# Products of 64 by 64 in the statistics pass of a four-layer convolution kernel

## The chip, the cores and the metric

The kernel runs on one core of a Trainium2 chip. The metric is the device time of one execution in microseconds, as the median of several runs. Beside it there is one profiled execution, from which every duration below is taken; a profiled execution can take a little longer than the others.

## The reference

The input is 4 images of 16 channels, 512 by 512, float32. Four layers follow one another: a window attention block with a small MLP (layer 0), a quantised 3x3 convolution with batch normalisation (layer 1), two 3x3 convolutions with a residual (layer 2), and a 3x3 convolution with a 16-128-16 MLP and a residual (layer 3). The change concerns layer 1 alone:

```python
def _L1_conv_ref(x, weight, gamma, beta):
    xq = _fake_quant(x, 8, 1.0)            # round(x / step) * step, step = max|x| / 127
    wq = _fake_quant(weight, 8, 1.0)
    y = conv3x3(xq, wq)                    # 16 -> 16 channels, padding 1
    mean = jnp.mean(y, axis=(0, 2, 3))     # per channel, over all images and pixels
    var = jnp.var(y, axis=(0, 2, 3))
    inv = gamma * jax.lax.rsqrt(var + 1e-5)
    y = y * inv[None, :, None, None] + (beta - mean * inv)[None, :, None, None]
    return jnp.clip(y, 0.0, 6.0)
```

The mean and variance of y need the whole of y before any pixel can be normalised. So the kernel computes y twice: once for its statistics alone, and once more in the pass that goes on through layers 1 to 3.

## The kernel before

The kernel has three stages. `window_attention` computes layer 0 and writes its result x1 to device memory, with a running maximum of its magnitude in `peak`. The statistics pass, in the first half of `conv_layers`, reads x1 once, convolves it and keeps only sums. A long loop over t (the second half of `conv_layers`) reads x1 again and runs layers 1, 2 and 3 in a pipeline to the output. An `attention_block` for inputs that the first form can't take is in the program but is branched over here.

How rows are laid out: x1 is a tensor of M + 1 = 65 blocks, each of 128 partitions x 4 strips (S) x 512 columns. A quarter of the partitions, `_quad(b)` = partitions 32b to 32b + 31, belongs to image b; within it 2 neighbouring rows (a pair) x 16 channels. Block mm holds pair mm of each of the 4 strips of the image. A 3x3 convolution of a pair needs two neighbouring blocks, `side` 0 and 1, and three column shifts `dx`; the weights `cq[_quad(b), side, dx, :]` are a 32 x 32 matrix (2 rows x 16 channels in, 2 rows x 16 channels out), the same in each quarter, in bf16, made by `quant_weights`.

The statistics pass runs over mm = 0 to 63. For one step:

- `scaled(mm + 2)` (L996) multiplies a loaded block by 1/step and adds a rounding constant, in place, on GpSimd (POOL; the first two blocks on VectorE).
- `rounded(mm + 2)` (L999) subtracts the constant on ScalarE (ACT) and writes bf16 into one of the three buffers `qs`, each with a zero column at either end.
- `_conv_turn` (L909) issues the products. `_turns` lists 24 turns (2 sides x 3 shifts x 4 images i), and each turn has 4 products, one for each strip j: rows of image i in the partitions `_quad(i)`, the output in `p[i][_quad(j)]`. So a step has 96 products of a 32 x 32 weight with 32 x 512 data, six of them accumulated into each 32 partitions x 512 columns of PSUM. A product is two instructions on TensorE, a weight load (PEld in the profile) and a matmul (PE). p is one of two sets of four PSUM banks, in turn, so that bank p[i] holds image i, all four strips.
- four `bn_stats` on VectorE (DVE, L1024), one a bank, reduce 512 columns of each partition to statistics in `stats`.
- `load` (L892) fetches block mm + 8 on SP's DMA queue into one of eight flat tiles, which are the buffers y, xi and x of the later loop. It waits until `rounded` has read that tile.

After the last step `bn_aggr` combines the statistics of each partition, `over_strips` adds the partitions of one channel (partition number modulo 16) through a product with the matrix `same`, and scale and shift of the normalisation follow. Which image or strip a partition of `stats` came from doesn't matter, only its channel.

The order on TensorE, VectorE, ScalarE and SP is the order in which the program is written (`tc.manual_schedule`); semaphores between engines come from what each instruction reads and writes. The main loop uses `_conv_turn` and `cq` too, from `group` (conv `None`), for the second computation of y.

Of the kernel before, what the change touches and what calls it, by code (L numbers as in the profile page):

```python
# [1 line left out]

# [10 lines left out]
BF16 = mybir.dt.bfloat16  # L13
# [10 lines left out]
B, C, H, W = 4, 16, 512, 512  # L24
P = 128
# [88 lines left out]
def conv_chain(ctx: ExitStack, tc: tile.TileContext, x, xw, mats, vecs, cqs, cws, hots, out):  # L114
# [33 lines left out]
    with tc.If(safe == 0):  # L148
        attention_block(tc, x, x1, m, v, peak)
    conv_layers(tc, x1, out, cw, cq, sw, m, v, peak)  # L150


# [728 lines left out]
def _quad(i):  # L881
    return slice(32 * i, 32 * i + 32)
# [18 lines left out]
def _turns():  # L901

    return [(side, dx, i) for side in range(2) for dx in range(3) for i in range(4)]


def _conv_turn(nc, p, weights, src, side, dx, i):

    for j in range(4):
        nc.tensor.matmul(  # L909
            p[i][_quad(j)], weights[_quad(i), side, dx, :],  # L910
            src[side][_quad(i), j, dx : dx + W],
            start=side == 0 and dx == 0, stop=side == 1 and dx == 2,
        )
# [3 lines left out]
def conv_layers(ctx: ExitStack, tc, x1, out, cw, cq, sw, m, v, peak):  # L917
# [18 lines left out]
    nc = tc.nc  # L936
    ld = ctx.enter_context(tc.tile_pool(name="l3l", bufs=2))
    act = ctx.enter_context(tc.tile_pool(name="l3a", bufs=1))
# [7 lines left out]
    def ring(name, n, dt=F32):  # L946
        tiles = rings[name] = [
            act.tile([P, 4, WP], dt, name=f"{name}{i}") for i in range(n)
        ]
        return lambda mm: tiles[mm % n]  # L950
# [5 lines left out]
    qs = ring("q", 3, BF16)  # L956
# [31 lines left out]
    def load(mm, t=None):  # L988
        if t is None:
            t = ld.tile([P, S, W], F32, tag="x", name=f"tx{mm}")  # L990
        loaded[mm] = t
        _load_pairs(nc, loaded[mm], x1, mm)

    def scaled(mm, at=slice(0, S), engine=nc.vector):
        t = loaded[mm][:, at]
        engine.tensor_scalar(t, t, ix, ROUND, ALU.mult, ALU.add)  # L996

    def rounded(mm, at=slice(0, S)):
        nc.scalar.activation(  # L999
            inner(qs(mm))[:, at], loaded[mm][:, at], AF.Identity, bias=unround  # L1000
        )

    flat = [
        t.rearrange("p s x -> p (s x)")[:, 0 : S * W].rearrange("p (s x) -> p s x", x=W)
# [9 lines left out]
    for mm in range(M):  # L1016
        if mm + 2 <= M:
            scaled(mm + 2, engine=nc.gpsimd)
            rounded(mm + 2)
        p = banks[4 * (mm % 2) : 4 * (mm % 2) + 4]  # L1020
        for turn in _turns():
            _conv_turn(nc, p, cq, (qs(mm), qs(mm + 1)), *turn)
        for b in range(B):
            nc.vector.bn_stats(stats[:, mm * B + b, :], p[b])  # L1024
        if mm + AHEAD <= M:
            load(mm + AHEAD, flat[mm % AHEAD])
# [166 lines left out]
    for t in range(-2, M + 7):  # L1193
# [5 lines left out]
        mm = t - 4  # L1199
# [5 lines left out]
        mm = t - 3  # L1205
# [7 lines left out]
        mm = t - 1  # L1213
# [4 lines left out]
        mm = t  # L1218
# [135 lines left out]
```

## Time and profile before

| | |
|---|---|
| median of 3 runs | 6459.06 us (6456.72 to 6465.38) |
| the profiled execution | 6479.63 us, span 6477.8 us |
| mean granted TensorE clock, whole span | 0.979 |
| TensorE busy, whole span | 6215.1 us, 96% |
| VectorE, ScalarE, GpSimd busy | 3208.4, 4062.8, 130.9 us |
| pairs of weight load and matmul | 146,976, of these 6144 in the statistics pass |
| end of the last product of the attention stage, start of the first of the statistics pass | 3541.8 us, 3577.3 us |
| last matmul of the statistics pass | begins at 3829.9 us |
| mean granted TensorE clock, 3577.2 to 3830.5 us | 0.71 |
| bytes moved and DMA share, 3577.2 to 3830.5 us | 267 GB/s, 0.71 |

Times within the span are counted from its start. "PE busy" is the union of the time in which matmuls were in flight; many are in flight at once, so that it doesn't tell how full the array is. "clock" is the share of TensorE's full clock that was granted. In the groups of instructions the columns are: line, engine, operation, what is written and read, rows*columns of the weight, count, then busy us and mean ns of one, then idle us of the engine before them with what ended it. "issue" is time in which the engine waited for nothing that the profile shows. A line of the DMA view is a queue: packets, MB, share of the time of 16 DMA engines.

### The profile page before, as it was taken

What the parts mean: (1) busy time and instruction counts of PE and PEld (TensorE: products, weight loads), DVE (VectorE), ACT (ScalarE), POOL (GpSimd) and SP (SyncE); (2) the same over time, 40 slices, a digit from 0 to 9 for tenths busy, and PEclk for the clock granted to TensorE, in tenths of its full rate; (3) what the DMA queues carried; (4) which work ended last, traced back from release to release, by engine and by line L of the source; (5) the groups of instructions that cost most, each with busy time, mean ns of one, the idle gap of its engine ahead of it and who ended that gap; (6) DMA issues with size and microseconds to landing.
All of it is one profiled execution on the core that took longest, in us unless ns stands there. A gap on an engine that the chain in (4) does not pass through costs nothing. (4 is left out here: it accounts for less than half of the span.)

```text
span 6477.8 us, 317011 instructions
## 1 busy us (share of the span) xinstructions
PE 6215.1 (96%) x146976; PEld 3422.4 (53%) x146976; DVE 3208.4 (50%) x4713; ACT 4062.8 (63%) x5602; POOL 130.9 (2%) x89
## 2 busy tenths in 40 slices
PE   8999999999999999999998569999999999999999
PEld 4555555555555555555553335555555555555554
DVE  3444444444444444444443564555555555555555
ACT  4777777777777777777775443444444444444444
POOL 0000000000000000000000520000000000000000
PEclk9999999999999999999998679999999999999999
DMA  3333333333333333333232752222222222222221
GB/s 80 62 72 61 72 61 72 61 72 61 72 61 72 60 73 61 72 60 73 59 58 36 295 181 75 83 82 82 83 84 86 81 81 81 81 86 82 83 74 51
DMA packets 568966, 515.30 MB, mean 80 GB/s; under 512 B 349008, under 2 KB 480208, under 8 KB 547152
## 3 DMA queue, kind: packets, MB, share of 16 engines
q1 hardware_dynamic: 567344, 494.52, 29.4%
q8 instruction: 1154, 18.91, 1.2%
q14 instruction: 180, 1.47, 0.1%
q10 hardware_dynamic: 288, 0.39, 0.0%
HBM read 225.87 MB, written 134.48 MB: 56 GB/s over the span
## 5 line engine op out<-in xcount | busy, mean ns | idle before, releaser
L1139 PE MATMUL tb<-y,mat 32*32 32x512 f32 x16384 | 1494.9, 596 | 6.5 <-issue 6.0
L1145 ACT ACTIVATE hid<-tb,vec 128x512 f32<-128x512 f32 x1280 | 829.5, 688 | 1068.3 <-PE tb L1139 1066.1
L368 ACT ACTIVATE e<-pair 128x1024 f32<-128x1024 f32 x1024 | 992.3, 1021 | 225.7 <-PE pair L360 225.0
L296 PE MATMUL pair<-x,taps 32*32 32x512 f32 x18432 | 968.2, 606 | 1.8 <-ACT y L307 1.2
L1147 DVE TENSOR_SCALAR hid<-tb,vec 128x512 f32<-128x512 f32 x768 | 574.4, 748 | 745.1 <-PE tb L1139 737.3
L417 PE MATMUL bank<-y,fc_e 32*32 32x512 f32 x8192 | 878.5, 607 | 3.7 <-ACT hid L422 3.1
L422 ACT ACTIVATE hid<-bank,f1b 128x512 f32<-128x512 f32 x1024 | 679.4, 686 | 298.4 <-PE bank L417 284.7
L352 DVE COPY yt<-bank 128x512 f32<-128x512 f32 x512 | 353.7, 691 | 905.6 <-PE bank L347 905.6
L360 PE MATMUL pair<-g,y 32*128 32x128 f32 x16384 | 652.1, 285 | 39.7 <-ACT e L368 38.7
L909 PE MATMUL tb<-z,cw 32*32 32x512 f32 x12864 | 634.6, 599 | 5.3 <-issue 4.1
L360 PEld LDWEIGHTS pair<-g,y 32*128 32x128 f32 x16384 | 541.4, 186 | 186.0 <-ACT e L368 108.8
L296 PEld LDWEIGHTS pair<-x,taps 32*32 32x32 f32 x18432 | 459.2, 103 | 288.5 <-issue 183.6
L1139 PEld LDWEIGHTS tb<-y,mat 32*32 32x32 f32 x16384 | 464.1, 103 | 270.7 <-issue 152.5
L909 PE MATMUL tb<-h,cw 32*32 32x512 f32 x12672 | 571.1, 597 | 3.5 <-ACT z L1078 1.5
L909 PE MATMUL tb<-q,cq 32*32 32x512 bf16 x12672 | 424.2, 458 | 151.3 <-issue 98.9
L909 PE MATMUL tb<-x,cw 32*32 32x512 f32 x12480 | 562.5, 597 | 2.0 <-ACT z L1078 1.4
L379 PE MATMUL bank<-e,yt 128*32 128x128 f32 x16384 | 555.3, 276 | 0.9 <-ACT r L394 0.9
L384 PE MATMUL bank<-e,hot 128*32 128x512 f32 x4096 | 534.4, 592 | 0.0
L379 PEld LDWEIGHTS bank<-e,yt 128*32 128x32 f32 x16384 | 417.7, 109 | 108.1 <-DVE yt L352 52.8
L1155 PE MATMUL tb<-hid,mat 128*32 128x512 f32 x4096 | 452.7, 594 | 0.0
L430 DVE TENSOR_TENSOR xo<-bank,y 128x512 f32<-128x512 f32 x256 | 177.0, 691 | 546.6 <-PE bank L428 544.7
L347 PEld LDWEIGHTS bank<-mat,y 128*128 128x128 f32 x2048 | 215.1, 141 | 430.1 <-issue 376.5
(158 smaller groups left out, 6731.7 us busy)
## 6 DMA issues: line engine op xcount, KB each, us to landing
x<-in_xw_dram SPq DMA_DIRECT2D x32, 2600.0 KB, 10.2
y<-y SPq DMA_DIRECT2D x2048, 32.0 KB, 2.1
tx<-x SPq DMA_DIRECT2D x64, 1024.0 KB, 5.7
xi<-x SPq DMA_DIRECT2D x1024, 64.0 KB, 2.1
out_dram<-xi SPq DMA_DIRECT2D x64, 1024.0 KB, 5.9
x<-xo SPq DMA_DIRECT2D x2000, 32.0 KB, 1.7
y<-x SPq DMA_DIRECT2D x24, 1024.0 KB, 5.5
xi<-x SPq DMA_DIRECT2D x24, 1024.0 KB, 5.2
```

The lines of the kernel that those rows point to most:

```text
L296: nc.tensor.matmul(bank(u)[quad(vv)], taps[quad(u), tap, :], xts[n // 2][quad(u), vv, dy : dy + WS, at : at + BW], start=tap == 0, stop=ta ...
L360: nc.tensor.matmul(bank(u)[:, P * jj : P * jj + P], y2[quad(u), vv, jl + jj].rearrange("p w t -> p (w t)"), g[quad(u), vv, jl + jj].rearra ...
L368: nc.scalar.activation(e[:, 2 * i : 2 * i + 2].rearrange("p u j t -> p u (j t)"), pairs[i], AF.Exp,)
L379: nc.tensor.matmul(b[quad(u), P * jj : P * jj + P], yt[:, jj, quad(u)], e[:, u, jj, :], start=True, stop=True,)
L384: nc.tensor.matmul(d[quad(u)], own, e[:, u].rearrange("p j t -> p (j t)"), start=True, stop=True,)
L417: nc.tensor.matmul(b[quad(k)], fc1[quad(vv), quad(k)], y[quad(vv), u, :], start=True, stop=True,)
L422: nc.scalar.activation(hd, b, AF.Gelu, bias=f1b)
L909: nc.tensor.matmul(p[i][_quad(j)], weights[_quad(i), side, dx, :], src[side][_quad(i), j, dx : dx + W], start=side == 0 and dx == 0, stop= ...
L1139: nc.tensor.matmul(p[_quad(c)], w1[_quad(b), 1 - par, 32 * c : 32 * c + 32], inner(ys(mm + par))[_quad(b), s, :], start=True, stop=True,)
L1145: nc.scalar.activation(hd, p, AF.Relu, bias=v("l3_b1"))
L1147: nc.vector.tensor_scalar(hd, p, v("l3_b1"), 0.0, ALU.add, ALU.max)
L1155: nc.tensor.matmul(p[_quad(b), :], w2[:, par], hd, start=par == 0, stop=par == 1)
```

## The change

The products of the statistics pass are formed over 64 rows and 64 columns. A new tile `cqs` holds, for each side and dx, a 64 x 64 matrix in each half of the partitions: the weights of one image in rows and columns 0 to 31, the same weights for the next image in rows and columns 32 to 63, and zeros elsewhere. It is filled once, by a memset and four copies on VectorE, just before the first loads of the pass.

A product takes two images at once (h picks images 0, 1 or 2, 3), one strip (2i + c), and writes 64 partitions, c picking the lower or upper half, of bank p[2h + i]. A step has 2 x 3 x 2 x 2 x 2 = 48 products instead of 96. A bank then holds two images of two strips in place of one image of four strips; each partition still belongs to the same channel as before. The main loop, the loads, the scaling, the rounding and the bn_stats are as they were. All else in the kernel is unchanged.

```diff
+import itertools
...
+    cqs = act.tile([P, 2, 3, 64], BF16, name="cqs")
+    nc.vector.memset(cqs, 0.0)
+    for i in range(4):
+        at = 32 * (i % 2)
+        nc.vector.tensor_copy(cqs[_quad(i), :, :, at : at + 32], cq[_quad(i)])
...
         p = banks[4 * (mm % 2) : 4 * (mm % 2) + 4]
-        for turn in _turns():
-            _conv_turn(nc, p, cq, (qs(mm), qs(mm + 1)), *turn)
+
+
+        for side, dx, i, h, c in itertools.product(range(2), range(3), *[range(2)] * 3):
+            nc.tensor.matmul(
+                p[2 * h + i][64 * c : 64 * c + 64], cqs[64 * h : 64 * h + 64, side, dx, :],
+                (qs(mm), qs(mm + 1))[side][64 * h : 64 * h + 64, 2 * i + c, dx : dx + W],
+                start=side == 0 and dx == 0, stop=side == 1 and dx == 2,
+            )
         for b in range(B):
             nc.vector.bn_stats(stats[:, mm * B + b, :], p[b])
```

## The prediction

> **What bounds the kernel now.** I read the page's strip of 40 slices first. TensorE is at 9 or 8 tenths everywhere but in slices 22 and 23 (each 162 us), and there the clock drops and the DMA rises. That is the statistics pass, the only place that the change touches.
>
> ```profile
> PE   8999999999999999999998569999999999999999
> PEclk9999999999999999999998679999999999999999
> DMA  3333333333333333333232752222222222222221
> ```
>
> The view of the weight tile `cq` puts its first matmul at 3577.3 us and the last at 3829.9, so with that one's 0.6 the pass takes 253.2 us for 64 steps (`mm`): 3.96 us a step. Next, the busy time by stage (busy and count of each engine, clock, DMA share, GB/s), in the part with saturated loads and the steady part:
>
> ```profile
> 3600.00:3620.00 20.00, 12.07 (x464) 7.72 (x444) 10.21 (x17) 9.07 (x5) 15.90 (x9) 0.51 1.01 417
> ...
> 3620.00:3815.00 195.00, 112.95 (x4688) 74.07 (x4657) 120.50 (x196) 96.30 (x49) 92.90 (x51) 0.73 0.69 255
> ```
>
> No engine is full in the steady part: TensorE 113 of 195 us, VectorE 120, and the DMA at 0.69 moves 255 GB/s where it moved 417 just before. So something waits on a latency. The groups of this pass say for whom:
>
> ```profile
> L1024 DVE BATCH_NORM_STATS2 h<-tb 128x6 f32<-128x512 f32 x256 | 158.6, 684 | 96.5 <-PE tb L909 95.8
> L909 PE MATMUL tb<-q,cq 32*32 32x512 bf16 x6144 | 150.0, 534 | 138.5 <-issue 98.9 <-ACT q L999 38.9 <-DVE h L1024 0.4
> L999 ACT ACTIVATE q<-y,unround 128x2048 bf16<-128x2048 f32 x25 | 49.5, 2002 | 79.1 <-PE tb L909 37.8 <-DVE y L996 37.7 <-POOL y L996 3.3
> ```
>
> VectorE and ScalarE wait for TensorE, and TensorE for "issue", nothing that the profile shows (the 38.9 on ScalarE is the start, almost all before the pass's first matmul). TensorE's timeline shows the rhythm:
>
> ```profile
> 3605.19 3.65 PE L909 MATMUL tb<-q,cq 32*32 32x512 bf16 x128 [3.07 <-issue]
> 3611.40 3.64 PE L909 MATMUL tb<-q,cq 32*32 32x512 bf16 x128 [2.57 <-issue]
> 3617.34 3.60 PE L909 MATMUL tb<-q,cq 32*32 32x512 bf16 x128 [2.29 <-issue]
> 3622.46 2.06 PE L909 MATMUL tb<-q,cq 32*32 32x512 bf16 x128 [1.52 <-issue]
> ```
>
> It stops after exactly 128 matmuls, although a step has 96: the stops belong to the instruction stream, not to the data. The DMA view gives the reason. On the page the instruction queue moved 18.91 MB in 1154 packets, 16.4 KB each. A product is a weight load and a matmul; all 146,976 such pairs are 293,952 instructions, and 18.91 MB over the 317,011 of the program is some 60 bytes each, so 128 pairs fill one packet. Packet times put the stops to the wait for such a packet:
>
> ```profile
> q8 instruction: 1154, 18.91, 1.2%
> ...
> q8 instruction: 37, 0.61, 1.2%
> ```
>
> The second line is 3620 to 3815: 37 packets, and 4688 / 128 = 36.6 blocks of matmuls. So a block costs 195 / 36.6 = 5.3 us, however long its arithmetic takes. With no loads in flight (after 3815) blocks start 3.5 to 4.0 us apart, with saturated loads (3593 to 3617) 5.9 to 6.2, at most 7.3 (3800.11 to 3807.43): instruction packets queue behind 1 MB loads. This is a reading of timings, not a wait that the profile names.
>
> **The change part by part.** (1) *Removed: half the pairs.* 64 steps x 96 = 6144 become 64 x 48 = 3072, 48 blocks become 24. At 5.3 to 6.2 us a block, fetching needs 2.0 to 2.3 us a step instead of 4.0, and it goes on while a block runs: at light load the packet starts about 1.06 us after the first matmul of the block before. So it stops being the bound if a block's arithmetic lasts longer than its fetch.
>
> (2) *Added: array time.* Full and half clock show in two stretches of one block (of these products alone: TensorE, weight loads, VectorE, then clock, DMA share, GB/s):
>
> ```profile
> 3617.40:3620.40 3.00, 3.00 (x128) 2.23 (x128) 0.00 (x0) 0.50 0.96 399
> ...
> 3655.70:3657.30 1.60, 1.60 (x127) 1.47 (x128) 0.00 (x0) 1.00 0.74 302
> ```
>
> At clock 1.00 a whole block is 2.06 us, of which 0.37 is the last matmul's own length; seven intervals between eight waves of 16 plus the starts in the last wave make the other 1.68, some 0.216 us a wave. At 0.50 it is 3.64 with 0.63 for the last: 0.431 a wave. A 64x64 product fills four of the sixteen sub-blocks, so a step is 48 / 4 = 12 waves instead of 96 / 16 = 6: 2.59 us at full clock, 5.17 at half. The trace has no 64x64 product. Bounds: four abreast at the bf16 wave, 216 / 4 = 54 ns each, from below; from above the row of 128x32 products, which also run four abreast but in f32:
>
> ```profile
> L1155 PE MATMUL tb<-hid,mat 128*32 128x512 f32 x4096 | 452.7, 594 | 0.0
> ```
>
> 452.7 us / 4096 = 110 ns, hence 48 x 110 = 5.3 us. I take 54, the row of the same type and line; that L1155 overlaps four products of 594 ns at 110 each tells me that column tiles of one row group run side by side.
>
> (3) *The clock.* It is 0.71 over the pass, since TensorE idles two fifths of it. Stages where TensorE is 99% busy (1000 to 1100, 5000 to 5100) have 0.99 to 1.00. With 12 waves a step TensorE has no pause unless something else stops it, so I take 1.00 after the first steps. From 3577.3 the first two run cold in part: conv(0) 5.2 us, conv(1) about 3, so 8.2 together.
>
> (4) *What is late next.* VectorE's four bn_stats took 2.49 us in a row (3685.81), and a set of banks is needed again two steps later; a 1 MB load (1.049 MB at the 420 GB/s of 3577 to 3620) 2.50; ScalarE's rounding 2.00; GpSimd's scaling 1.97. All lie just under 2.59. Rounding of mm+2 can begin when conv(mm-1) has read its third buffer, and is needed in the second half of conv(mm+1): some two steps for 2.0 us. SP's loads go out after the rounding, eight steps ahead; nothing moves on SP or POOL. A block is 128 / 48 = 2.67 steps, 6.9 us at full clock, against 5.9 to 6.2 for a fetch under saturated loads: hidden by 0.7 to 1.0. If it were not, each further us costs 0.37 a step. With three servers within 4% of each other I add 0.11 for the times when one is late: 2.70 a step.
>
> (5) *Building cqs on VectorE:* a 128x384 memset and four 32x192 copies. The memset of 128x512 f32 took 485 ns, the 32x32 copies 172: about 1.4 us in all. They stand before the quantisation step; VectorE then sat idle for 3.74 us until 3573.85 for the first load, so they cost nothing; without that cover, 1.4 us.
>
> *Sum.* 8.2 + 62 x 2.70 = 175.6 us for the pass in place of 253.2: 77.6 off. The profiled execution took 6479.6 (span 6477.8), so 6402 by its own time. The median, 6459.1, is 20.5 below it. If the profiler's cost lies outside this pass the median falls to 6381.5; if all of it sits in this pass, which is bound by a DMA latency, only 57 are to be had, 6402. I take 74 off: 6385.
>
> [...]
>
> **The rivals.**
> (a) *The fetch stays the bound.* Loads would now run at 0.97 of the DMA instead of 0.69, and packets might wait as long as in the worst interval, 8.4 us (3584.95 to 3593.31). Then 8.4 / 2.67 = 3.15 a step, 8.2 + 62 x 3.15 = 203, 50 off: 6409. For it: the spread of 4.0 to 7.3. Against: the saturated stretch had 5.9 to 6.2.
> (b) *The clock stays mixed*, at 0.71: 2.59 / 0.71 = 3.65 a step, 234 us, 19 off: 6440. For it: any stop of 2 us brought 0.5 for some us. Against: the busy stages.
> (c) *Slower: the clock stays at half, or the tiles run two abreast.* One price: 5.17 us a step, 331 in place of 253, 78 on: 6537. It decides from 3.96 us a step, 330 ns for a wave of four. For it: the pass starts at 0.50, and kept it for 20 us (3600 to 3620); no 64x64 row. Against: there TensorE was idle 40% of the time, and at half clock it would be the only bound and never idle, the state in which every other stage shows 1.00.
> (d) *The change does not touch the bound:* if the stops were set by data loads, a step would stay near 3.96, and the time within a few us of 6459. Against: stops every 128, and a DMA at 0.69.
>
> **How the numbers follow.** Forecast 0.75, (a) 0.11, (b) 0.03, (c) 0.08, (d) 0.03. Below, the loads set the limit: 2.50 a step is 90 off, 6369; I begin at 6368. Above, (a) with a little of the profiler's share: 6413. Slower by over 0.2% (13 us; about what this kernel's runs can tell) is (c) and a part of (d): 0.09; within 0.2%: 0.03; faster 0.88.
>
> **What would show it.** Matmuls `q,cqs` x3072, 64x512, at a median near 375 to 400 ns; 12 waves near 216 ns; clock near 1.00 from about 3590; "issue" before them under 20 us instead of 98.9; the pass ending near 3753; loads at about 0.95 of the DMA; VectorE's bn_stats almost back to back; 24 instruction packets fewer. Wrong if the clock stays under 0.8, if waves of four take over 300 ns, or if stops after 128 pairs last 2 us and more.

## The result, and the profile after

The changed kernel takes 6390.38 us (median of 4 runs, 6387.1 to 6395.64) against 6462.22 for the one before (4 runs, 6456.72 to 6470.9): 71.8 us less, ratio 0.9888 with a 95% interval of 0.9871 to 0.9906. The forecast was 6385.

The page's strips of the changed kernel, 40 slices of 160 us, in tenths:

```profile
PE   8999999999999999999999789999999999999999
PEclk9999999999999999999999899999999999999999
DMA  3333333233323233333322752222222222222221
```

The dip in slices 22 and 23 is almost gone from TensorE and its clock; what is left is the time between the stages, before the first load has arrived and after the last statistics. Two stretches of the pass (busy and count of TensorE, weight loads, VectorE, ScalarE, GpSimd; clock, DMA share, GB/s):

```profile
3590.00:3620.00 30.00, 30.00 (x562) 21.26 (x558) 28.76 (x47) 23.27 (x12) 23.82 (x13) 1.00 1.01 419
...
3660.00:3700.00 40.00, 40.00 (x745) 30.47 (x741) 38.44 (x62) 30.82 (x16) 30.76 (x16) 1.00 1.01 419
```

TensorE is full at clock 1.00, VectorE at 96%, and the DMA moves 419 GB/s where it moved 255. TensorE's whole pass is now two lines of its timeline:

```profile
3570.23 6.25 PE L1030 MATMUL tb<-q,cqs 64*64 64x512 bf16 x72 [35.41 <-ACT q L1000]
3579.52 162.44 PE L1030 MATMUL tb<-q,cqs 64*64 64x512 bf16 x3000 [3.04 <-ACT q L1000]
```

After 1.5 steps it waits 3.04 us for a block that ScalarE is still rounding, and then 3000 products run without one gap: no stop after 128. The groups say the same (idle before, and what ended it), and so does the instruction queue on the page, with 24 packets fewer than 1154:

```profile
L1030 PE MATMUL tb<-q,cqs 64*64 64x512 bf16 x3072 | 168.7, 379 | 38.5 <-ACT q L1000 38.5
L1036 DVE BATCH_NORM_STATS2 h<-tb 128x6 f32<-128x512 f32 x256 | 159.5, 686 | 14.3 <-PE tb L1030 7.8
```

```profile
q8 instruction: 1130, 18.51, 1.3%
```

"issue" is no longer among what TensorE's matmuls wait for, and VectorE's wait for them fell from 95.8 to 7.8 us.

Where the time went, from the two traces: the pass from 253.0 to 171.7 us (81.3 less), what follows it from 2647.6 to 2647.1, and the pass began at 3570.2 instead of 3577.3. Those last 7.1 us lie in code that the change doesn't touch; in the executions below with full loads the pass began anywhere from 3573.9 to 3581.9. So the spans differ by 88.8, the medians by 71.8: the first profiled execution of the kernel before was a long one.

### The profile page after: what moved, and what is told of

The parts are those of the page before. It is cut to its first block, busy times and chain, and to the rows that moved or that the text cites. A ratio compares the mean times of both kernels' runs of the same rounds, so it can differ in the third digit from the quotient of the medians.

```text
span 6389.0 us, 310874 instructions
## 1 busy us (share of the span) xinstructions
PE 6228.6 (97%) x143904; PEld 3444.3 (54%) x143904; DVE 3210.5 (50%) x4718; ACT 4065.0 (64%) x5602; POOL 130.9 (2%) x89
## 5 line engine op out<-in xcount | busy, mean ns | idle before, releaser
L396 DVE TENSOR_TENSOR o<-bank,r 128x512 f32<-128x512 f32 x512 | 354.4, 692 | 141.5 <-ACT r L395 122.6
```

## The experiments

For each run, from its trace: pairs of weight load and matmul in a step, the pass from the first matmul's start to the last one's end, the mean step after the third, and the mean distance of the starts of blocks of 128 pairs where TensorE stops after them. Each experiment is one execution. The kernel before, executed beside them, took 6469.1 to 6475.3 us, and its two profiled passes below differ by 7.3 us, so a few us more or less in a pass mean nothing.

| run | pairs a step | pass, us | step, us | block, us |
|---|---|---|---|---|
| before | 96 | 253.0 | 3.96 | 5.29 |
| after | 48 | 171.7 | 2.60 | no stops |
| before_again | 96 | 245.7 | 3.86 | 5.19 |
| split256 | 96 | 245.4 | 3.76 | 5.41 |
| split128 | 192 | 428.9 | 6.61 | 4.57 |
| before_quarter | 96 | 196.2 | 3.05 | 4.18 |
| before_strips | 96 | 260.3 | 4.07 | 5.41 |
| half_products | 48 | 162.9 | 2.53 | two stops, 1.8 us in all |
| after_quarter | 48 | 169.4 | 2.60 | no stops |

**The kernel before, once more.** No edit.

> The kernel before, unchanged, profiled a second time. The first profiled execution took 6479.6 us where its other runs had a median of 6462. If the statistics pass is what varies (a latency that depends on what else the DMA does), this execution differs from the first by the length of its pass, which was 253.2 us; if the difference lay elsewhere, the pass is again 253 within 3 us and the attention stage, which ended 7 us later in the first than in the changed kernel, gives the rest.

It took 6464.8 us, 14.8 less than the first profiled execution. The pass was 7.3 us shorter and the loop after it 12.0 (2635.6), while the pass began 4.3 us later. So neither answer held alone: about half of the first execution's excess lay in the pass. Against this execution the changed pass saves 74 us rather than 81.

**The count put back, with the array time of the changed kernel.**

```diff
-        for side, dx, i, h, c in itertools.product(range(2), range(3), *[range(2)] * 3):
+        for n, side, dx, i, h, c in itertools.product(
+            range(2), range(2), range(3), *[range(2)] * 3
+        ):
+            at = 256 * n
             nc.tensor.matmul(
...
+                p[2 * h + i][64 * c : 64 * c + 64, at : at + 256],
+                cqs[64 * h : 64 * h + 64, side, dx, :],
+                (qs(mm), qs(mm + 1))[side][
+                    64 * h : 64 * h + 64, 2 * i + c, at + dx : at + dx + 256
+                ],
...
```

> The changed kernel with each 64x512 product cut into two of 256 columns: 96 pairs of weight load and matmul in a step again, the same array time (24 waves of half the length, about 2.6 us a step at full clock), the same tiles. Theory, the instruction packets set the pace: a block of 128 pairs is again 1.33 steps, its arithmetic some 3.5 us against 5.3 to 6.2 us for a packet, so TensorE stops after each 128 and a step takes about 4.0 us, the pass some 255 us. Rival, the wide tiles or the steady clock did it and the count doesn't matter: 2.6 to 2.7 us a step, pass 172 to 180 us, no stops.

The pass took 245.4 us, where the unchanged kernel's run above took 245.7: the whole gain is gone with the same wide tiles. TensorE's timeline and the busy time of a stretch (columns as above) of this run:

```profile
3702.06 3.70 PE L1033 MATMUL tb<-q,cqs 64*64 64x256 bf16 x128 [1.69 <-issue]
3707.45 3.70 PE L1033 MATMUL tb<-q,cqs 64*64 64x256 bf16 x128 [1.69 <-issue]
3711.74 10.92 PE L1033 MATMUL tb<-q,cqs 64*64 64x256 bf16 x384 [0.59 <-issue]
3724.90 5.36 PE L1033 MATMUL tb<-q,cqs 64*64 64x256 bf16 x128 [2.23 <-issue]
```

```profile
3620.00:3800.00 180.00, 137.87 (x4572) 127.56 (x4576) 119.00 (x192) 94.77 (x48) 94.38 (x48) 0.96 0.79 284
```

The groups hold 128 or a multiple of 128, and after each TensorE waits for "issue". Three blocks in a row without a stop (x384 in 10.9 us) show that a packet can be in time at 3.6 us a block; on the average it isn't. The clock is 0.96 here, against 0.71 in the kernel before, and the pass is no shorter: the low clock doesn't make the stops. That the stops make the low clock is likely, but no rule comes out of it: in the kernel before, each of the 26 stops of 2.07 us or more was followed by a mean clock of 0.67 or less in the next 4 us, in this run 5 of the 10 such stops. This fells the rival that wide tiles or a steady clock made the gain.

**192 pairs a step.** As above with `range(4)` and 128 columns.

> The changed kernel with each product cut into four of 128 columns: 192 pairs in a step, the array time in streaming unchanged. Theory, packets of 128 pairs set the pace: 1.5 blocks a step; the loads then need only half the DMA's time, so a block comes every 4.2 to 5.4 us, 6.3 to 8.1 us a step, twice that of 96 pairs. Rival, the loads or something else per step sets the pace: near 4 us as with 96 pairs.

6.61 us a step, inside the theory's range and far from the rival's 4. The stops of this run:

```profile
3706.67 2.00 PE L1033 MATMUL tb<-q,cqs 64*64 64x128 bf16 x128 [2.02 <-issue]
3711.51 3.05 PE L1033 MATMUL tb<-q,cqs 64*64 64x128 bf16 x128 [2.84 <-issue]
```

At full clock a block has 2.00 us of arithmetic here, like the 2.06 of 32x32 products, and as many instructions, and it starts 4.57 us after the one before. With the loads at 146 GB/s it is shorter than the 5.2 to 5.4 of 96 pairs.

**Fewer bytes to queue behind.** The loads of the pass cut to one strip of four; the other strips hold a constant that rounds to zero.

```diff
+        if quarter:
+            s = int(mm == M)
+            nc.sync.dma_start(t[:, 0:1], x1[mm - s * M, :, s : s + 1])
+            return
...
+        nc.vector.memset(flat[mm][:, 1:S], ROUND)
...
-            scaled(mm + 2, engine=nc.gpsimd)
+            scaled(mm + 2, slice(0, 1), engine=nc.gpsimd)
```

> The kernel before, with the loads of the statistics pass cut to one strip of four (256 KB in place of 1 MB; the other three strips are filled once with the rounding constant, so that they round to zero), the scaling cut to that strip, and all 96 products of a step kept. Theory, instruction packets queue behind the loads: blocks of 128 pairs come every 3.5 to 4.0 us as where no loads were in flight, 2.6 to 3.0 us a step, and TensorE still stops after 128. Rival, the instruction stream is slow by itself: 5.3 us a block and 4.0 us a step, unchanged.

```profile
3705.73 2.06 PE L909 MATMUL tb<-q,cq 32*32 32x512 bf16 x128 [2.51 <-issue]
3709.47 2.23 PE L909 MATMUL tb<-q,cq 32*32 32x512 bf16 x125 [1.69 <-issue]
...
3713.49 3.27 PE L909 MATMUL tb<-q,cq 32*32 32x512 bf16 x128 [1.19 <-issue]
```

The step fell from 3.86 to 3.05 with every product kept, and TensorE's timeline still stops after 128 (the second block's last three products waited 0.20 us for VectorE and stand in the line left out). So the loads lengthen the wait and don't make it: with a quarter of the bytes a block still costs 4.18 us, a little over the 4.0 that I took for the upper end (and 3.05 a step over 3.0).

**The same bytes in smaller rows.** Each load as four DMAs of a strip (`t[:, s]` from `x1[mm, :, s]`).

> The kernel before, with each load of the pass issued as four DMAs of one strip: rows of 2 KB in place of 8 KB, the same bytes. If an instruction packet waits behind a number of data packets, packets of a quarter of the size let it through sooner: blocks of 128 pairs near 4.2 us as with quarter loads, 3.1 us a step. If it waits behind bytes that are queued, whatever their pieces: 5.2 us a block, 3.9 us a step, unchanged.

The packets did become smaller, as the DMA view of 3620 to 3780 says (23439 in place of 5782 on the loads' queue for the same 42 MB):

```profile
DMA packets 23472, 43.18 MB, mean 270 GB/s; under 512 B 2603, under 2 KB 2603, under 8 KB 23439
...
q1 hardware_dynamic: 23439, 42.68, 83.2%
```

The block took 5.41 us and the step 4.07, no less than in the two runs of the kernel before (5.29 and 5.19, 3.96 and 3.86). So an instruction packet doesn't wait behind a fixed number of data packets; waiting by bytes fits. More than that these runs don't show of the queue.

**Half the products, 32x32 as before.** Only side 0; the products of side 1 are left out.

> The kernel before, with only the 48 products of side 0 in a step, 32x32 as before; the products of side 1 are left out. Theory: a block of 128 is 2.67 steps, a packet of 5.9 to 6.2 us under saturated loads gives 2.2 to 2.3 us a step, so the loads (2.50 us) and VectorE (2.49) set the pace: 2.5 to 2.6 us a step, with three waves of arithmetic only, and loads near 420 GB/s. Rival, a wait in each step (a semaphore, a buffer) rather than in each 128 instructions: stays between 3.5 and 4.0 us.

```profile
3600.00:3740.00 140.00, 85.80 (x2656) 37.73 (x2671) 136.50 (x223) 110.40 (x55) 109.03 (x58) 0.50 1.01 418
```

2.53 us a step, as the theory had it. This stretch ran at half clock throughout and with TensorE busy 61% of the time, and still a step took 2.5: the loads at 418 GB/s or VectorE at 97% set it, and the run doesn't part the two. What it leaves out halves the array time together with the count, so by itself it can't say which of the two matters; the two runs above that cut the products finer change the count and keep the array time nearly as it is. The step of 2.53 is the floor under the changed kernel, and 64 x (2.60 - 2.53) is under 5 us; I tried no version for it.

**What paces the changed kernel.** Its loads cut to a quarter, as above.

> The changed kernel with the loads of the pass cut to one strip of four (256 KB; the other strips hold the rounding constant and round to zero) and the scaling cut to that strip; all 48 products kept. Theory, TensorE's twelve waves now set the pace: 2.59 to 2.60 us a step, unchanged, at a quarter of the DMA's rate. Rival, the loads (2.50 us at 420 GB/s, the DMA busy throughout) set it: the step falls to VectorE's 2.4 to 2.5 us or lower.

```profile
3600.00:3730.00 130.00, 130.00 (x2410) 99.08 (x2406) 124.84 (x201) 101.68 (x51) 35.91 (x52) 1.00 0.40 106
```

2.60 us a step at 106 GB/s, as with full loads: TensorE's twelve waves set the step, and not the loads, though in the changed kernel they keep the DMA busy 1.01 of the time.

**The same products where packets are in time.** The main loop's second convolution with 64x64 products too.

```diff
...
+            elif wide:
+                side, dx, j, h = next(pairs)
+                for c in range(2):
+                    nc.tensor.matmul(
+                        conv_banks[2 * h + j][64 * c : 64 * c + 64], cqs[64 * h : 64 * h + 64, side, dx, :],
+                        conv[1][side][64 * h : 64 * h + 64, 2 * j + c, dx : dx + W],
...
-        weights = cq if layer is None else cw[:, layer]
+        weights = cqs if layer is None else cw[:, layer]
```

> The changed kernel with the 64x64 products also in the main loop's second computation of the quantised convolution (68 turns of it, 48 pairs in place of 96; a bank then holds other images and strips than the next layer takes it for). There blocks of 128 pairs already last 4.9 to 5.1 us at 83 GB/s of data, so packets are in time. Theory: array time counts, six more waves of 0.216 us a turn, and 68 x 1.3 = 88 us more than the changed kernel's main loop (2636 to 2647 us from the end of the pass), more still if TensorE loses time between products of 32 and of 64 rows, which alternate there. Rival, the main loop too is paced by its instruction stream, or half the count is worth having everywhere: 3264 fewer pairs at 5.0 us for 128 are 125 us less.

It took 6727.03 us, against 6472.0 for the kernel before beside it. The loop after the pass took 2978.9 us instead of 2639.9 (after_quarter, the same loop). The sign was the theory's, the size four times as large. Its timeline shows why:

```profile
5016.19 1.06 PE L1151 MATMUL tb<-y,mat 32*32 32x512 f32 x8
5017.18 0.41 PE L1192 MATMUL tb<-q,cqs 64*64 64x512 bf16 x4
5017.52 1.06 PE L1151 MATMUL tb<-y,mat 32*32 32x512 f32 x8
5018.51 0.41 PE L1192 MATMUL tb<-q,cqs 64*64 64x512 bf16 x4
```

The second column is how long a group was in flight: each begins when the one before is all but over (the second at 5017.18, the first ends at 5016.19 + 1.06 = 5017.25). With one size, in the changed kernel, products of the two lines share the array: four `q,cq` products begin at 5031.11 us while 18 of the hidden layer's last until 5031.69, and the next of those begin at 5031.31, before the four end at 5031.52. With two sizes they take turns, each group beginning some 0.07 us before the end of the one before. Two more runs tested that: the sets of hidden products first, and the wide ones after them, so that the size changes twice in a turn instead of ten times; and the narrow products in that order as a control.

```diff
             conv(None, qs, mm, done0, mm) if -2 <= mm <= M + 1 else None,
-            (t - 5, 1) if 0 <= t - 5 < M else None, [], EARLY,
+            (t - 5, 1) if 0 <= t - 5 < M else None, [], range(8),
```

> As the kernel with 64x64 products in the main loop too, but in that group the eight hidden sets (32x32 products in f32) are issued first and the 24 turns of 64x64 products after them, so that the two sizes change once in a group instead of ten times; the output is again that of other strips. That kernel's main loop took 2979 us, 340 more than the 2640 of the others, where array time gave 88. Theory, TensorE does not overlap products of one size with those of another, and each change of size costs: the loop comes back to the time of the narrow kernel in the same order plus 88 to 130 us. Rival, the 64x64 products are themselves dear beside f32 work: still 300 us and more above the narrow one.

> Control for the run above: the changed kernel with 32x32 products in the main loop, the group's hidden sets first and its conv turns after them. The hidden sets, four products abreast, then share the array with nothing of their own group: the main loop takes 0 to 150 us more than 2640 (32 products of four abreast at 0.11 us are 3.5 us a turn at most, some 0.43 us of it still shared, less where conv turns then run undisturbed).

The loop took 2733.2 us with wide products (span 6478.3) and 2661.5 with narrow ones (span 6412.7): 71.7 us apart, 1.05 a turn, under the 88 of six whole waves. The narrow kernel lost 21.6 us by that order (2661.5 against 2639.9), inside the 0 to 150 expected; the wide one won 2978.9 - 2733.2 = 246 us, so that much came from alternating. Idle time of the weight loads before wide products, ended by "issue", fell with it, in the view of L1192 (us, times), first alternating and then apart:

```profile
  issue: 361.0, 624
```

```profile
  issue: 62.9, 87
```

## Why the prediction was right

*The bound.* That TensorE waited for 16.4 KB packets of its own instructions was an inference from packet times. It is now borne out by the count: restored without the old tiles (split256, pass back at 245), doubled again (split128, 429), and, with the array time, halved without the new tiles (half_products, 163). The packets' times in the traces say the same stop by stop: in the six runs of the table that stop all along, each of the 298 stops that end in "issue" ends 1.2 to 1.6 us after an instruction packet has come in, whether that packet began 1.1 us after the first matmul of the block before or 5.7. The profile names no such wait, but nothing on record is left beside it: (d), a bound that the change doesn't touch, fell with half_products (the same loads, 2.53 us a step), and (b) with split256, slow at clock 0.96.

One working of it was loose: some 60 bytes an instruction came from dividing the packets' bytes by the instructions of all engines. The result counts it better: 24 packets fewer for 6144 instructions fewer are 256 instructions, or 128 pairs, in each.

*Part (1).* 24 packets fewer, as counted, and no stop left: 2.67 steps of 2.60 are 6.9 us a block, against the 5.9 to 6.2 from block to block in the kernel before, behind loads at 417 GB/s. Rival (a) saw the loads saturate as it said (1.01, more than the 0.97 it had), but packets were in time nonetheless. Its price was too high besides: the 8.4 us that it took for the worst interval hold 219 products and not 128; the longest block that the first trace shows is the 7.3 of 3800.11 to 3807.43, which would give 2.74 a step.

*Part (2).* 54 ns was the right end. 62 steps of 2.59 to 2.60 us are twelve waves of 0.216; the bound of 110 ns from L1155 was far off. In the trace the products start in fours, 0.215 to 0.220 us from one four to the next: the tiles of both halves run four abreast, so (c) did not come about.

*Part (3).* The clock was at 1.00 from 3574.7 on, where the second step begins (3575.0); I had the second step still cold in part. That idle time lowers the clock is my reading and no more: it was 0.71 with TensorE idle for 41% of the pass in the kernel before, 0.50 with 39% in half_products, 0.96 with 23% in split256.

*Part (4).* The allowance of 0.11 a step was mis-sized: after the second step nothing was late, 62 x (2.70 - 2.595) = 6.5 us too much, although three servers stood within 4% of each other. The start was mis-sized the other way: 10.6 us for the first two steps instead of 8.2, since TensorE waited 3.04 us for the third rounded block, a wait that the kernel before had too (2.48 us at 3584.95) and that I had left out. Together 175.6 forecast, 171.7 measured: two errors of opposite sign, of which the first was the larger.

*Part (5).* The fill of `cqs` cost nothing on the path: VectorE still sat idle for 2.50 us until the first load had landed, in place of 3.74. Its own price was 1.0 us, not 1.4:

```profile
L1009 DVE COPY cqs<-cq x4: 198/201/206, 3562.3 to 3562.9; 32x192 bf16<-32x192 bf16 x4
L1006 DVE MEMSET cqs<- x1: 218/218/218, 3562.0 to 3562.0; 128x192 uint32 x1
```

*From profile to median.* Taking 74 off the median rather than 77.6 was a choice between two ends; before_again shows it to have been of the right kind, with some 7 of the 14.8 us of excess inside the pass. That 74 is also what the changed pass saves against before_again is in part luck: the forecast pass was 3.9 us too long, the first measured pass some 7 us longer than the second, and one choice between 57 and 77.6 covered both. The measured 71.8 lies between these ends.

*The price in array time.* Six waves a step became twelve. In the kernel before, the products of a block at full clock start in sixteens, 0.215 to 0.226 us apart (the block at 3655.62); in the changed one, in fours. Where TensorE waited for packets that cost nothing: blocks whose products last 2.0 to 5.4 us left the stops of the six runs, and those of 6.9 us left none. In the main loop, where TensorE is busy 99% of the time, the wide products cost 71.7 us (wide_apart against narrow_apart).

## What to carry to other kernels

If TensorE stops at fixed counts of instructions and not of steps (here 128 pairs, with 96 in a step), suspect that it waits for its program, as it did here: count instructions, not only array time. Larger products paid here although half of their weights are zeros, 2.60 us a step in place of 3.96, since a block of 128 pairs then lasted 6.9 us and its packet was in time. The same edit in the main loop, where 128 pairs already take 5.1 us and TensorE waits for "issue" for 6.5 us in all after 3780, was a loss of 71.7 us. Before widening products, look whether others of another size are interleaved with them: alternating the two cost 246 us more there.

## What the runs showed of the hardware that was not expected

- Products of different tile sizes did not share the array (wide_main, above): alternating them ten times a turn instead of two cost 246 us over the 61 turns that have both, 0.50 us for each of 488 further changes.
- A block of 128 pairs was never nearer than 3.47 us to the one before where TensorE stopped between them, in any of these runs, though its arithmetic took as little as 2.0 us.
- Rows of 2 KB instead of 8 KB in the data loads brought the instruction packets no sooner (5.41 us a block against 5.29 and 5.19), but raised the DMA's busy share from 0.71 to 0.83 for the same bytes.
- At clock 0.50 and busy 61% of the time, TensorE kept a step of 2.53 us (half_products): there the low clock did not mean that TensorE was the bound.
